# A two-layer selective-scan block: a new load and head, constants made by GpSimd, and unread products on TensorE

## The chip, the cores and the metric

The kernel runs on one core of one Trainium2 chip. The metric is the device time of one execution in microseconds (us), the median of several runs; lower is better. Names used below: TensorE (PE; its weight loads are PEld in the profile), VectorE (DVE), ScalarE (ACT), GpSimd (POOL) and SyncE (SP, which here only issues DMAs). SBUF is the on-chip memory and PSUM the accumulator memory that TensorE writes, which this kernel takes in banks of 512 floats per partition.

## The reference

The input x is an image of 64 x 64 pixels with 96 channels, so L = 4096 tokens. Two layers of the same kind follow each other, each with a residual connection:

```
x = x + conv_block_0(group_norm(x))
x = x + conv_block_1(group_norm(x))

# a block, d = 192 inner channels, n = 16 states
xz = x @ in_proj                      # 96 -> 2 * 192
x_val, z = split(xz)
x_val = silu(depthwise_conv_3x3(x_val))
# four orders of the tokens (by rows, by columns, each forward and backward)
for each order s:
    dt, B, C = split(s @ x_proj)      # 6, 16, 16
    dt = softplus(dt @ dt_proj + bias)
    h[t] = h[t-1] * exp(dt * A) + dt * s * B      # 192 x 16 states
    y_s = sum_n h * C + s * D
y = layer_norm(sum of the four y_s, put back in order) * silu(z)
return y @ out_proj
```

Layer 0 writes its scan as a cumulative sum divided by a decay with 1e-12 added, so that what lies far from the start of an order is swamped and only its first steps count. Group norm has 32 groups of 3 channels.

## The kernel before

Tokens lie along the free dimension and channels on the partitions. The 192 inner channels by 4096 tokens are three blocks of 128 partitions by 2048 columns; a partition half of 64 holds 64 channels for one half of the 512-token chunks.

**Load** (L155 to 163): eight transfers bring x in tiles of 128 tokens by 4 by 96; TensorE turns them four at a time into a PSUM bank, and DVE copies the bank to xT (96 x 4096). Four `xt` buffers are in rotation. DVE also makes the constants from the identity (L95 to L142: `fold`, `fold2`, `wide`, `i3`, `selh`, `less`). `selh` is a bf16 selection matrix, 96 x 1024: a product with 128 of its columns as weights spreads a row of B over 128 partitions.

**Head** (`head`, once a layer): bn_stats (L1347 in layer 0, L1322 behind the residual in layer 1), bn_aggr (L1141), a small product `pm` (L1143) that averages over the groups, three DVE steps, a product `pv` (L1149), Ln and Exp on ACT for the reciprocal deviation `rs`, and eight DVE instructions for the normalised `xn` (L1156). `project` and `borders` (L1163, L1181) are the in-projection; ACT copies it into a padded image (L1167, L1185). The depthwise convolution has twelve parts (three blocks by four chunks): DVE does blocks 0 and 1, two chunks at a time, as nine scaled additions (`conv`, L1237 and L1239); TensorE does block 2, chunk by chunk, as nine products with diagonal weights (`conv_by_products`, L1216). `finish` applies SiLU and starts y. `gate` (L1193 to L1199) computes silu(z) in twelve parts, `sz`, and stores them in DRAM through three buffers.

**Near part** (`near_scans`, layer 0): only the first 192 steps of each order are computed. TensorE selects the tokens (`nu`, L276 to L289), projects them (`npj`, L300), and expands dt (`npd`, L334). ACT and DVE make softplus of it (Abs, Exp, Identity, Ln at L347 to L350, then L351 to L354). Nine bf16 products spread B over the partitions (`nB`, L412 and L414, four PSUM banks, of which 2048 columns are there and the last 256 are free). Six units follow, two for each block: ACT makes decays (`nna`) and weights (`nnwt`), DVE multiplies B and du into `nb` (L467, L474) and scans (L475), POOL multiplies by C (L480), TensorE sums over the states (`ny`, L494), and DVE adds to y after every second unit (L518). After the second unit `reach` (L388 to L399) computes a flag that says whether 192 steps are enough, by a transpose `worst` (L397); the full scans of layer 0, `far_scans`, stand behind a branch on that flag and don't run on this input.

**Tail**: layer norm, the product with silu(z) and the out-projection with the residual.

**Layer 1's scans** (`scans`; nearly all of the span): eight groups of 24 units. All operations go through `Ordered`, a helper that keeps the written order on each engine, so the profile gives all of them the line L668 of that helper. The first group has a start of its own (`first`): `pj` projects, `xd` copies, `pd` expands dt, `tB` transposes B, then on ACT four softplus steps for each of three blocks (`wl`, `w`), with the copy `BT` of tB and the decays `am` (L226) after the second block's steps, then `a` (stage_a), the casts of B to three bf16 parts with the products `less` between, and the transposes `tu`. After that DVE's scans (`h`) run.

What sets the order: outside `Ordered` parts and `keep_in_program_order` the order on an engine is chosen by a scheduler from due times; every engine runs its own queue in order. A reader of a tile waits for the last write to that tile that stands ahead of it in the program, so tiles that share a PSUM tile share waits.

```
            ps = pps.tile([128, 4, 512], F32, tag="B", name="npd")[:, 0:3, 0 : 2 * NEAR]
...
            nc.scalar.activation(w, ps, AF.Abs)
...
                    ps = me["ps"] = spare(f"tB{k}", "v" if k else "b0")
```

Of the kernel before, what the change touches and what calls it, by code (L numbers as in the profile page):

```python
# [16 lines left out]
HW = 64  # L17
L = HW * HW
DM = 96
# [24 lines left out]
def two_ss2d_layers(  # L44
# [43 lines left out]


    load_exp_ln()  # L90
    ident = const.tile([128, 128], F32, name="ident")
    make_identity(nc, ident)

# [5 lines left out]
    for half in HALF:  # L99
        nc.vector.tensor_add(fold[:, half], ident[:, HALF[0]], ident[:, HALF[1]])  # L100
    fold2 = const.tile([128, 128], F32, name="fold2")
    nc.vector.tensor_scalar_mul(fold2, fold, 0.5)

    wide = []
    for h in range(2):
        t = const.tile([128, 128], F32, name=f"wide{h}")
        nc.vector.memset(t, 0.0)
        for half in HALF:
            nc.vector.tensor_copy(t[HALF[h], half], ident[HALF[h], HALF[h]])
        wide.append(t)  # L110
# [9 lines left out]
    nc.sync.dma_start(out=gav, in_=gavg)  # L120
# [4 lines left out]
    nc.vector.tensor_add(i3, ident[0:NB, 0:32], ident[0:NB, 32:64])  # L125
    nc.vector.tensor_add(i3, i3, ident[0:NB, 64:96])
    selh = const.tile([NB, NS, 2, 64], BF16, name="selh")
    for h in range(2):
        nc.vector.tensor_copy(
            selh[:, :, h, :],  # L130
            i3.rearrange("p (q two) -> p q two", two=2)[:, :, h]
            .unsqueeze(2)
            .to_broadcast([NB, NS, 64]),
        )
# [7 lines left out]
    nc.vector.tensor_scalar_mul(less, ident[0:NB, 0:NB], -1.0)  # L142


    u = [pers.tile([128, L // 2], F32, name=f"u{T}") for T in range(3)]
    y = [pers.tile([128, L // 2], F32, name=f"y{T}") for T in range(3)]
    xs = dpool.tile([DM, L], F32, name="xs")
    szd = [dpool.tile([3, 128, L // 2], F32, name=f"szd{l}") for l in range(2)]


    xp = ExitStack()
    xT = xp.enter_context(tc.tile_pool(name="xT0", bufs=1)).tile([DM, L], F32, name="xT0")
    with tc.tile_pool(name="ld", bufs=4) as ld, tc.tile_pool(
        name="ldp", bufs=4, space=PSUM
    ) as ldp:  # L155
        xr = x.rearrange("(g j p) c -> g p j c", p=128, j=4)
        for g in range(8):
            xt = ld.tile([128, 4, DM], F32, tag="xt", name=f"xt{g}")
            (nc.sync if g % 2 == 0 else nc.scalar).dma_start(out=xt, in_=xr[g])
            pt = ldp.tile([DM, 512], F32, tag="pt", name=f"pt{g}")  # L160
            for j in range(4):
                nc.tensor.transpose(pt[:, j * 128 : (j + 1) * 128], xt[:, j, :], ident)
            nc.vector.tensor_copy(xT[:, g * 512 : (g + 1) * 512], pt)
# [82 lines left out]
    def near_scans(weights):  # L246
# [4 lines left out]
        WN = 4 * NEAR  # L251
        with ExitStack() as sc:
# [19 lines left out]
            for T in range(3):  # L272
                ps = pps.tile(
                    [128, 4 if T == 2 else 2, 512], F32, tag="ymB"[T], name=f"nu{T}"
                )[:, 0:2]
                nc.tensor.matmul(  # L276
                    ps[:, 0, 0:NEAR], wide[0], u[T][:, 0:NEAR], start=True, stop=True
                )
                nc.tensor.matmul(
                    ps[:, 0, NEAR : 2 * NEAR], wide[1], u[T][:, L // 2 - NEAR :][:, ::-1],  # L280
                    start=True, stop=True,
                )
                for h in range(2):
                    nc.tensor.matmul(
                        of_columns(ps[:, 1, 0:NEAR], h), wide[h],
                        columns(u[T], h, slice(0, k)), start=True, stop=True,
                    )

                    nc.tensor.matmul(  # L289
                        of_columns(ps[:, 1, NEAR : 2 * NEAR], 1 - h), wide[h],  # L290
                        columns(u[T], h, slice(HW - k, HW))[:, ::-1, ::-1, ::-1],
                        start=True, stop=True,
                    )
                (nc.scalar.copy, nc.vector.tensor_copy)[T % 2](us[:, T], ps[:, :, 0 : 2 * NEAR])
# [3 lines left out]
            for T in range(3):  # L298
                for q in range(2):
                    nc.tensor.matmul(  # L300
                        ps[:, q], xw[HALF[q], 0, T, :], us[HALF[q], T, q],
                        start=(T == 0), stop=(T == 2),
                    )
# [27 lines left out]
            ps = pps.tile([128, 4, 512], F32, tag="B", name="npd")[:, 0:3, 0 : 2 * NEAR]  # L331
            for T in range(3):
                for h, half in enumerate(HALF):
                    nc.tensor.matmul(  # L334
                        ps[half, T], dwb[96 : NC + 1, 0, T, half],
                        xd[96 : NC + 1, 2 * NEAR * h : 2 * NEAR * (h + 1)], start=True, stop=True,
                    )
            w, ln, t, v, sums = (
# [47 lines left out]
            def reach():  # L386
                for i, (n, m0, m1) in enumerate(kinds):
                    nc.vector.tensor_mul(  # L388
                        top[:, i],
                        S.rearrange("p t q (d w) -> p t (q d) w", w=NEAR)[:, :, :, n - 1],  # L390
                        most[:, i, :].unsqueeze(2).to_broadcast([128, 3, 4]),
                    )
                nc.vector.reduce_max(
                    most[:, len(kinds), 0:1], top.rearrange("p i a b -> p (i a b)"), axis=AX.X
                )
                ps = pps.tile([128, 2, 512], F32, tag="m", name="worst")
                nc.tensor.transpose(ps[0:1, 0, 0:128], most[:, len(kinds), 0:1], ident)  # L397
                nc.vector.reduce_max(most[0:1, len(kinds), 1:2], ps[0:1, 0, 0:128], axis=AX.X)
                nc.vector.tensor_scalar(flag, most[0:1, len(kinds), 1:2], GONE, None, ALU.is_le)  # L399
# [5 lines left out]
            for n, m0, m1 in kinds:  # L405
                B.append([])
                t = once.tile([128, m1 - m0, 4 * n], F32, name=f"ncb{n}")
                for m in range(m0, m1):
                    dst = Bf[:, at : at + 4 * n]
                    if n == NEAR:  # L410
                        for s in (slice(0, 512), slice(512, WN)):
                            nc.tensor.matmul(dst[:, s], pick(0, m), B3[:, s], start=True, stop=True)  # L412
                    else:
                        nc.tensor.matmul(  # L414
                            dst.rearrange("p (d w) -> p d w", w=n), pick(0, m),
                            parts(B3)[:, :, 0:n], start=True, stop=True,
                        )
# [5 lines left out]
                cb.append(t.rearrange("p n w -> p (n w)"))  # L423

# [58 lines left out]
            def add(j):  # L483
# [6 lines left out]
                for i in ks:  # L490
                    n, m0, m1 = kinds[i]
                    for m in range(m0, m1):
                        for q in range(2):
                            nc.tensor.matmul(  # L494
# [4 lines left out]
                            o += 2 * n  # L499
                if ks[0]:  # L500
# [153 lines left out]
    def scans(weights):  # L654
# [5 lines left out]
        class Ordered:  # L660
            def __init__(self, engine):
                self.engine = engine

            def __getattr__(self, name):
                op = getattr(self.engine, name)


                return lambda *args, **more: tc.keep_in_program_order(op(*args, **more))  # L668

# [3 lines left out]
        with ExitStack() as sc:  # L673
# [4 lines left out]
            load_exp_ln()  # L678
# [30 lines left out]
            def prelude(k):  # L709
# [48 lines left out]
                def tokens_B():  # L758

                    ps = me["ps"] = spare(f"tB{k}", "v" if k else "b0")  # L760
# [155 lines left out]
            def first(  # L916
# [6 lines left out]
                for h in range(2):  # L923
                    projected(h)
                rows()
                for begin, by_scalar, by_vector in parts:
                    begin()
                tokens_B()
                for T, (begin, by_scalar, by_vector) in enumerate(parts):
# [193 lines left out]
    def head(l, xT, w):  # L1123

        ipw_s, v, ds = w["ipw"], w["v"], w["ds"]
        with ExitStack() as sc:
# [12 lines left out]
            gst = cv.tile([DM, 6], F32, name=f"gst{l}")  # L1139
            gm, rs = gst[:, 2:3], gst[:, 5:6]  # L1140
            nc.vector.bn_aggr(gst[:, 0:2], w["st"].rearrange("p a b -> p (a b)"))  # L1141
            pm = cvp.tile([DM, 1], F32, tag="z", name=f"pm{l}", bufs=3)
            nc.tensor.matmul(pm, gav, gst[:, 0:1], start=True, stop=True)  # L1143
# [5 lines left out]
            nc.tensor.matmul(pv, gav, gst[:, 4:5], start=True, stop=True)  # L1149
            nc.scalar.activation(rs, pv, AF.Ln, bias=eps5[0:DM])  # L1150
            nc.scalar.activation(rs, rs, AF.Exp, scale=-0.5)

            xn = cv.tile([DM, L], F32, name=f"xn{l}")
            for g in range(8):
                s = slice(g * 512, (g + 1) * 512)
                nc.vector.tensor_scalar(xn[:, s], xT[:, s], gm, rs, ALU.subtract, ALU.mult)  # L1156
# [68 lines left out]
            def conv(b, s):  # L1225


                room = cw.tile([128, 2, SR, W2], F32, tag="acc", name=f"acc{l}_{b}_{s}")
                acc = room.rearrange("p c r w -> p c (r w)")[:, :, 0 : SR * W2 - 2]
                for k, (i, j) in enumerate(taps):  # L1230
                    o = i * W2 + j
                    src = pad[b].rearrange("p c r w -> p c (r w)")[
                        :, 2 * s : 2 * s + 2, o : o + SR * W2 - 2
# [6 lines left out]
                finish(b, slice(1024 * s, 1024 * (s + 1)), room[:, :, :, 0:HW])  # L1240
# [11 lines left out]
            conv(0, 0)  # L1252
            for c in range(NCH):
                conv_by_products(2, c)
            for b, s in ((1, 0), (0, 1), (1, 1)):
                conv(b, s)
# [88 lines left out]
    st = [pers.tile([DM, 8, 6], F32, name=f"st{l}") for l in range(2)]  # L1345
    for g in range(8):
        nc.vector.bn_stats(st[0][:, g, :], xT[:, g * 512 : (g + 1) * 512])  # L1347
    nc.sync.dma_start(out=xs, in_=xT)
    for l in range(2):
# [11 lines left out]
        nc.vector.reduce_sum(ds, v[:, :, V_D : V_D + 4], axis=AX.X)  # L1361
# [97 lines left out]
```

## Time and profile before

| | us |
|---|---|
| median of 3 runs | 1553.86 (1553.56 to 1554.03) |
| the profiled execution | 1545.96 |
| its span in the profile | 1543.8 |
| mean granted TensorE clock | 0.913 of full |
| DVE busy, whole span | 1354.3 (88%) |
| first scan of layer 0's near part (L475) | starts at 127.08 |
| tail of layer 0 (first m) | starts at 179.67 |
| bn_aggr of layer 1 | starts at 222.90 |
| first pj of layer 1 | starts at 289.95 |
| first scan of layer 1 (h) | starts at 317.03 |

A line of the timeline reads: start, busy time, engine, source line, operation, written tile <- read tiles, shape, and in brackets the idle time of that engine ahead of it with what ended it. Consecutive instructions of one kind are one line, and "x12" is their number; the busy time is then that of all of them. A matmul of floats is recorded as several passes, so that the records of TensorE are more than the products written in the code. The clock (PEclk) is the share of full speed that TensorE was granted; in short windows of this profile it is 0.50 or 1.00, and a mean over a longer window lies between. The profiled execution is one single run, some 8 us shorter than the median of the timed ones.

### The profile page before, as it was taken

The page shows a single profiled execution, that of the slowest core. Times are in us where ns is not written, and L with a number is a line of the kernel's source. Part 1 is how long each engine was busy: PE and PEld are TensorE (multiplying, and loading weights), DVE is VectorE, ACT ScalarE, POOL GpSimd, SP SyncE. Part 2 cuts the span into 40 slices and gives each one's busy share as a digit, 9 for nine tenths or more (in the row PEclk, how much of TensorE's full clock was granted, in tenths as well). Part 3 has the DMA queues.
Part 4 walks back from the last instruction along what each step waited for, and adds up shares of the span by engine and source line. Part 5 has one row for each costly group of instructions (what it writes and reads, how often), then busy time and mean ns, then how long its engine had stood idle before and what let it go on. Part 6 is the DMA issues. An engine that isn't in the chain of part 4 may idle for free.

```text
span 1543.8 us, 17370 instructions
## 1 busy us (share of the span) xinstructions
PE 1258.3 (82%) x5158; PEld 507.0 (33%) x5158; DVE 1354.3 (88%) x942; ACT 1196.7 (78%) x2459; POOL 1102.9 (71%) x593
## 2 busy tenths in 40 slices
PE   5953779798897888798888889797979888877778
PEld 3432424233332323232323333333333332322223
DVE  6936389469999999999999999999999999999976
ACT  3456125669989898898999999999898989897733
POOL 0032100149898999899898989898989899998860
PEclk8975689869999999998999999999999899999999
DMA  4031330441625344352626162526263544526223
GB/s 111 11 107 45 89 87 1 127 106 37 144 74 133 82 111 108 85 126 68 151 55 153 55 138 57 137 57 146 65 140 76 124 97 96 123 70 146 74 81 96
DMA packets 82674, 146.32 MB, mean 95 GB/s; under 512 B 31580, under 2 KB 33820, under 8 KB 82476
## 3 DMA queue, kind: packets, MB, share of 16 engines
q1 hardware_dynamic: 79884, 142.78, 38.2%
q0 software_dynamic: 576, 1.57, 0.4%
q10 hardware_dynamic: 2112, 0.79, 0.2%
q8 instruction: 42, 0.69, 0.2%
q14 instruction: 60, 0.49, 0.1%
HBM read 80.85 MB, written 12.13 MB: 60 GB/s over the span
## 4 chain that ended last, share of the span: by engine, by line
DVE 26%; issue 21%; PE 13%; ACT 11%; POOL 7%; DMA 6%; SPq 5%; DVEq 0%; POOLq 0%; ACTq 0%
DVE h L668 17%; DVE b L668 6%; POOL hc L668 5%; SPq L668 5%; ACT a L668 4%; PE ys L668 3%; ACT bT L668 2%; PE pj L668 2%; PE b L668 2%; PE cp L1216 2%; DMA cb<-C 2%; DMA du<-su 2%; DMA xT<-xs 1%; PE pd L668 1%; PE in L1163 1%
## 5 line engine op out<-in xcount | busy, mean ns | idle before, releaser
L668 POOL TENSOR_TENSOR hc<-h,cb 128x1024 f32<-128x1024 f32 x384 | 902.7, 2367 | 116.3 <-DVE h L668 61.8
L668 DVE TENSOR_TENSOR_SCAN h<-a,carry,b 128x1024 f32<-128x1024 f32 x288 | 665.2, 2337 | 30.3 <-PE b L668 6.4
L668 ACT ACTIVATE a<-dt,am 128x1024 f32<-128x1024 f32 x384 | 438.6, 1142 | 94.3 <-DVE h L668 91.3
L668 PE MATMUL ys<-hc,fold 128*64 128x512 f32 x1536 | 434.2, 645 | 2.6 <-POOL hc L668 2.6
L668 ACT ACTIVATE bT<-duT,BT 128x192 f32<-128x192 f32 x1012 | 387.2, 445 | 8.3 <-PE b L668 6.4
L668 PE MATMUL b<-ident,bT 128*128 128x128 f32 x1536 | 223.5, 289 | 34.3 <-DVE h L668 27.4
L668 DVE TENSOR_TENSOR b<-b,du 128x1024 f32<-128x1024 f32 x192 | 232.2, 1209 | 12.3 <-PE b L668 12.3
L668 PEld LDWEIGHTS b<-ident,bT 128*128 128x128 f32 x1536 | 176.6, 147 | 160.9 <-DVE h L668 99.1
L668 DVE TENSOR_TENSOR_SCAN h<-a,b 128x1024 f32<-128x1024 f32 x96 | 216.1, 2278 | 13.9 <-PE b L668 6.0
L668 PE MATMUL b<-B,selh 96*128 96x512 bf16 x384 | 122.4, 402 | 90.0 <-DVE h L668 89.9
L668 PEld LDWEIGHTS ys<-hc,fold 128*64 128x64 f32 x1536 | 79.0, 140 | 142.2 <-issue 102.8
L668 PEld LDWEIGHTS <-selh 96*128 96x128 bf16 x384 | 25.9, 98 | 220.9 <-DVE h L668 124.1
L668 PE MATMUL pj<-u,xw 64*124 64x512 f32 x192 | 94.2, 636 | 3.1 <-ACT sz L1198 1.7
L668 PE MATMUL pd<-xd,dwb 29*64 29x512 f32 x192 | 58.2, 677 | 47.0 <-DVE w L668 40.1
L1239 DVE SCALAR_TENSOR_TENSOR acc<-pad,v,acc 128x1052 f32<-128x1052 f32 x64 | 79.6, 1308 | 0.2
L668 POOL DMA_DIRECT2D du<-su x12 | 6.4, 538 | 81.7 <-ACT am L226 79.7
L668 PE MATMUL ys<-y,ident 128*128 128x512 f32 (+1 forms) x120 | 64.7, 646 | 0.0
L1216 PE MATMUL cp<-pad,diag 128*128 128x512 f32 x144 | 62.3, 593 | 0.0
L668 ACT CAST B<-pj 96x512 bf16<-96x512 f32 (+2 forms) x96 | 54.9, 575 | 4.5 <-PE pj L668 4.5
L668 POOL TENSOR_TENSOR sp<-sp,ln 128x512 f32<-128x512 f32 x45 | 57.4, 1275 | 0.2
L668 POOL TENSOR_TENSOR ln<-ln,w 128x512 f32<-128x512 f32 x45 | 57.4, 1276 | 0.0
L668 POOL TENSOR_TENSOR su<-sp,u 128x512 f32<-128x512 f32 x45 | 57.3, 1274 | 0.0
(173 smaller groups left out, 1173.7 us busy)
## 6 DMA issues: line engine op xcount, KB each, us to landing
cb<-C SPq DMA_DIRECT2D x256, 256.0 KB, 4.1
dt<-sp SPq DMA_DIRECT2D x192, 128.0 KB, 4.2
du<-su SPq DMA_DIRECT2D x180, 128.0 KB, 4.2
szd<-sz SPq DMA_DIRECT2D x24, 256.0 KB, 3.1
szt<-szd SPq DMA_DIRECT2D x24, 256.0 KB, 6.8
xT<-xs SPq DMA_DIRECT2D x8, 384.0 KB
xs<-xT SPq DMA_DIRECT2D x1, 1536.0 KB
xs<-xT SPq DMA_DIRECT2D x8, 192.0 KB, 2.3
```

Of the source, the lines that this page charges most:

```text
L668: return lambda *args, **more: tc.keep_in_program_order(op(*args, **more))
L1163: nc.tensor.matmul(ps[half], ipw_s[:, 64 * b : 64 * b + 64], xn[:, g * 512 : (g + 1) * 512], start=True, stop=True,)
L1216: nc.tensor.matmul(ps.rearrange("p (r w) -> p r w", w=HW), diag[:, k, :], pad[b][:, c, i : i + SR, j : j + HW], start=(k == 0), stop=(k == ...
L1239: nc.vector.scalar_tensor_tensor(acc, src, wk, acc, ALU.mult, ALU.add)
```

## The change

The load is written anew, and stands ahead of the constants: each partition reads 1536 contiguous bytes of x, there are eight buffers, ACT makes the copy to xT with a stride of four, and DVE takes bn_stats from PSUM:

```diff
+    with tc.tile_pool(name="ld", bufs=8) as ld, tc.tile_pool(
+        name="ldp", bufs=4, space=PSUM
+    ) as ldp:
+        xr = x.rearrange("(g p j) c -> g p j c", p=128, j=4)
...
+            (nc.sync if g % 2 == 0 else nc.scalar).dma_start(out=xts[g], in_=xr[g])
...
+                nc.tensor.transpose(pt[:, j], xts[g][:, j, :], ident)
+            nc.scalar.copy(
+                xT[:, g * 512 : (g + 1) * 512].rearrange("c (p j) -> c j p", j=4), pt
+            )
+            tc.keep_in_program_order(
+                nc.vector.bn_stats(st[0][:, g, :], pt.rearrange("c j p -> c (j p)"))
+            )
```

`fold`, `fold2`, the copies in `wide`, `i3`, `selh` and `less` go from nc.vector to nc.gpsimd. The transfer of `gav` and the store of xT stand behind that in the text. A new function issues products whose result nothing reads:

```diff
+    def warm(ps, n):
+        for i in range(n):
+            tc.keep_in_program_order(
+                nc.tensor.matmul(
+                    ps, pick(0, 0), selh.rearrange("p q a b -> p (q a b)")[:, 0 : ps.shape[-1]],
+                    start=True, stop=True,
+                )
+            )
```

They are called in the head, where xn is also split between DVE and ACT:

```diff
+            filler = cvp.tile([128, HT], F32, tag="ed", name=f"warm{l}")
+            warm(filler, 8)
             pm = cvp.tile([DM, 1], F32, tag="z", name=f"pm{l}", bufs=3)
...
+            warm(filler, 3)
...
+            warm(filler, 4)
             nc.scalar.activation(rs, pv, AF.Ln, bias=eps5[0:DM])
             nc.scalar.activation(rs, rs, AF.Exp, scale=-0.5)
+            nc.vector.scalar_tensor_tensor(shift, gm, -1.0, rs, ALU.mult, ALU.mult)
...
+                if g % 2 == 0:
+                    nc.vector.tensor_scalar(xn[:, s], xT[:, s], gm, rs, ALU.subtract, ALU.mult)
+                else:
+                    nc.scalar.activation(xn[:, s], xT[:, s], AF.Identity, bias=shift, scale=rs)
```

in the near part, whose products all go through `Ordered` now:

```diff
-            ps = pps.tile([128, 4, 512], F32, tag="B", name="npd")[:, 0:3, 0 : 2 * NEAR]
+            room = pps.tile([128, 4, 512], F32, tag="B", name="npd")
+            ps = room[:, 0:3, 0 : 2 * NEAR]
...
+            warm(room[:, 3], 32)
...
+            filler = Bf[:, 2048 - 256 :]
+            warm(filler, 110)
...
+                if j + 1 < len(units):
+                    warm(filler, 16)
```

and in layer 1's first group:

```diff
-            load_exp_ln()
             am = []
...
-                    ps = me["ps"] = spare(f"tB{k}", "v" if k else "b0")
+                    ps = me["ps"] = spare(f"tB{k}") if k else me["room"][:, halves[0]]
...
                     projected(h)
+                load_exp_ln()
                 rows()
                 for begin, by_scalar, by_vector in parts:
                     begin()
+                room = state[0]["room"] = pps.tile([128, TC], F32, tag="b0", name="room")
                 tokens_B()
+                warm(room[:, halves[1]], 30)
```

The last chunk of block 2's convolution goes from TensorE to DVE, as DVE's last one:

```diff
-            conv(0, 0)
-            for c in range(NCH):
+            conv(0, slice(0, 2))
+            for c in range(NCH - 1):
                 conv_by_products(2, c)
-            for b, s in ((1, 0), (0, 1), (1, 1)):
-                conv(b, s)
+            for b, c in ((1, 0), (0, 2), (1, 2)):
+                conv(b, slice(c, c + 2))
+            conv(2, slice(NCH - 1, NCH))
```

The sum `ds` of the skip weights moves from ahead of the head into it, behind xn.

## The prediction

> **What bounds the kernel.** I read the page's busy sums first, then the timeline of 0 to 346 us, then short windows with the granted clock.
>
> ```profile
> PE 1258.3 (82%) x5158; PEld 507.0 (33%) x5158; DVE 1354.3 (88%) x942; ACT 1196.7 (78%) x2459; POOL 1102.9 (71%) x593
> DVE  6936389469999999999999999999999999999976
> PEclk8975689869999999998999999999999899999999
> ```
>
> DVE is full from the tenth slice on (layer 1's scans), and the change doesn't touch those. It touches the first nine slices, where DVE waits. So each edit is priced by how far it moves the chain there; a delay or a gain at the first scan of layer 1 (317.03) goes to the end unchanged, because DVE has no slack behind it. The chain, from the timeline:
>
> ```profile
> 16.51 4.24 DVE L1347 BATCH_NORM_STATS2 st<-xT 96x6 f32<-96x512 f32 x7
> 20.79 0.37 DVE L1141 BATCH_NORM_AGGREGATE gst<-st 96x2 f32<-96x48 f32 x1
> 32.02 0.77 DVE L1237 TENSOR_SCALAR acc<-pad,v 128x1052 f32<-128x1052 f32 x1 [4.68 <-ACT pad L1185]
> 89.06 0.59 PE L276 MATMUL nu<-u,wide 128*128 128x192 f32 x2 [1.62 <-ACT sz L1198]
> 102.44 1.13 ACT L347 ACTIVATE nw<-npd 128x1152 f32<-128x1152 f32 x1
> 111.64 0.80 PE L412 MATMUL nB<-nB,selh 96*128 96x512 bf16 x2 [9.24 <-DVE nv L353]
> 121.51 0.97 DVE L467 TENSOR_TENSOR nb<-nB,ndu 128x768 f32<-128x768 f32 x1 [2.35 <-DMA ndu<-ndu]
> 126.02 0.96 DVE L474 SCALAR_TENSOR_TENSOR nb<-nnwt,nb 128x768 f32<-128x768 f32 x1 [0.49 <-ACT nnwt L447]
> 153.59 5.38 PE L494 MATMUL ny<-nnhc,fold 128*128 128x64 f32 x24 [1.05 <-POOL nna L453]
> ```
>
> Each line gives the start, the busy time and, in brackets, the idle time ahead of it with what ended it. The reader is to see which lines follow each other without slack (102.44 stands 0.03 behind the end of npd at 102.41) and which have some (nB ends at 113.3, and the nb that reads it starts at 121.51): an added wait costs its length less that slack. In the last line PE is the late one: DVE's y add waits until 159.01 for these 24 products.
>
> **Part by part** (shifts in us against before; negative is earlier).
>
> 1. Load. Before, DVE makes constants (6.42 to 9.2), copies and then does seven bn_stats in 4.24, and the second half of the transposes starts at 12.22. After, all eight transfers are issued at once and DVE only does bn_stats from PSUM, behind ACT's copy. PE is then the bound: 16 transposes took 3.62, so 32 take 7.2 from about 4.0; with a copy (0.6 like ACT's pad rows) and a bn_stats (0.68) the aggregate starts at 12.8 instead of 20.79: **-8.0**. Ends: 11.5 (transposes partly at full clock) to 15.7 (the stride-4 copy on ACT at twice its 0.6, eight of them in line); I take 0.6 because nothing shows a slower one. The constants on POOL lie under this: POOL has 14.63 us idle before its pads, against some 3 us of DVE work moved to it; only selh is wanted soon, by the first filler. On SP's queue gav is still second and the store of xT falls one place back, behind small weight loads that nothing reads before 96 us; the last two transfers of x wait for the first two to land (4.49), 5 us ahead of their transposes. If they came 2 us late, that is inside the upper end.
>
> 2. Norm. Eight unread products stand before pm and wait for the last bn_stats; 512-column bf16 products took 0.43 at half clock and half of that at full, so 8 take 1.7 to 3.4, of which 0.4 to 0.5 lies under the aggregate. The three and four fillers behind pm and pv delay pv and the first `in` product only if they outlast DVE's four small steps (0.78) and ACT's Ln, Exp and shift (1.04): 1.3 and 1.7 at half clock, so up to 0.5 each, none at full. The added DVE shift costs 0.2 (rows of 96x1: 0.15). The diag products on ACT (2.74, nine) now follow its copies and end near 15, ahead of pv. **+2.2** (+1.2 to +4), -5.8 in all.
>
> 3. xn to conv. 23.61 to 32.02 is 8.41. Four xn go to ACT (0.6 each), which delays its pads, and the clock, half until 29.6, should be full earlier: 7.0 (6.5 to 9). **-1.4**, -7.2.
>
> 4. Conv to nu. 57.0 before: PE runs the conv products of block 2 (36, as 72 records, 43.05 to 74.2), then z; sz is bound by its stores to 89.0. After, 54 records (23.4), so z starts 7.8 sooner, at conv start + 34.3, and the 14.9 us from z to nu end at +49.2. DVE gets one more conv of half width: 0.45 and eight of 0.69 to 0.74 (the 128x512 rows of layer 1) are 6.3, so it ends at 42.6 + 6.3 = +48.9, then SiLU and y on ACT. The two are level, and what is late next is ACT: u (1.15) and y (1.15) of the last blocks stand among the twelve sz, and npj needs all of u. I take 51.2. **-5.8** (-2.5 to -7.8), -13.0.
>
> 5. 32 products behind npd. They write the fourth bank of npd's PSUM tile, and the built program's instruction list shows that ACT's Abs (102.44) now waits for the last of them, not for the last npd. Abs had started 0.03 after npd. Queued behind it on ACT are Exp, Identity, Ln, the next table load and the dt copies, and DVE's nv chain waits for those; nothing else on the path can run meanwhile. Four us at half clock (9), the rest at full: **+8.9** (6.8 all full, 13.7 all half). The 9.24 us of idle PE before nB stay, so the clock is not kept.
>
> 6. 110 products behind nB, in nB's tile: DVE's first nb (121.51) waits for the last. nb may start as late as 125.05 without delaying 126.02. Nine nB products take 1.66, then about 11 fillers of 256 columns at 0.21 and 99 at 0.107: nB + 15 to 16 = 127.0. **+1.7** (0 to +11.8 if all are at 0.21).
>
> 7. Near units. 24 small ny at half clock (0.224 each) took 5.38 and DVE waited 5.19, 4.18 and 8.45 for them. At full clock they would take about 3.1 (0.13 each: at 151.82, with the clock full, four weight loads of the same kind took 0.52). Against that, sixteen fillers of 256 columns (1.7 to 3.4) after each unit but the last stand on PE before the worst transpose (DVE's reduce and all its later nb wait there) and before the next ny, and as they write nB's tile, they wait for DVE's latest nb and the next nb for them. The keeping of program order on PE itself moves nothing here: the ny already ran in that order. **-3.3** (-4.5 to +3).
>
> 8. Layer 1's norm and conv: as 2 to 4, with xn split: **-1.4** (-2.6 to +0.5) and 55.4 becoming 50.4, **-5.0** (-2 to -6). In all -12.1 at pj (289.95).
>
> 9. First group.
>
> ```profile
> 298.39 1.06 PE L668 MATMUL tB<-ident,xd 32*128 32x32 f32 x8
> 300.57 0.24 ACT L668 COPY BT<-tB 128x128 f32<-128x128 f32 x1
> 301.77 0.60 ACT L668 ACTIVATE wl<-pd 128x512 f32<-128x512 f32 x1
> 306.15 1.15 ACT L668 ACTIVATE a<-dt,am 128x1024 f32<-128x1024 f32 x1 [1.75 <-DMA dt<-sp]
> 307.20 1.04 ACT L668 CAST B<-pj 96x512 bf16<-96x512 f32 x2
> 307.82 1.07 PE L668 MATMUL pj<-B,less 96*96 96x512 bf16 x2 [8.37 <-ACT B L668]
> 309.93 2.77 PE L668 MATMUL tu<-ident,su 128*128 128x128 f32 x12
> ```
>
> The 30 fillers share tB's tile, so the copy BT waits for the last: 299.45 + 8.5 = 308.0, 7.45 later. Behind it on ACT stand am, the third softplus, a, and the casts that less and tu need. a had 1.75 of idle, of which 1.5 is used: **+5.95** (+3.8 all full, +10.3 all half) and 0.13 for the table load, which stood under pj (289.92, ending 1.67 before xd could start) and now stands behind the two xd copies, where ACT had 1.16 of idle before wl for its 1.28. PE then idles some 6 us again until less. Could the clock stay full to 346, DVE's waits there (1.92 + 3.99 + 2.24 + 1.20) would mostly go, -8.
>
> ```profile
> core 0: us, PE busy (x) PEld busy (x) DVE busy (x) ACT busy (x) POOL busy (x), PEclk, DMA share, GB/s
> 104.00:111.00 7.00, 0.00 (x0) 0.00 (x0) 5.09 (x7) 4.45 (x4) 4.55 (x5) 0.50 0.49 135
> 111.60:113.40 1.80, 1.65 (x9) 1.00 (x9) 1.76 (x2) 0.47 (x1) 0.43 (x1) 0.50 0.07 6
> 316.90:322.40 5.50, 5.50 (x8) 1.86 (x8) 4.56 (x3) 1.72 (x4) 3.00 (x2) 0.50 0.60 161
> ```
>
> The third window has PE busy in all of its 5.50 us, on 64-row products, at clock 0.50: a busy PE was not enough, so I give no part of the 8. The Trainium skill ("TensorE: Matmul & The Clock Gate", Part 1) lifts the clock after about 3.4 us of sustained work, whatever it is; by that rule this window would have been lifted and the sum would be up to 8 lower. The row differs, and the row decides.
>
> **Sum**: -8.0 + 2.2 - 1.4 - 5.8 + 8.9 + 1.7 - 3.3 - 1.4 - 5.0 + 5.95 + 0.13 = -6.0. The profiled execution took 1545.96 us, 7.9 below the median of 1553.86; both move alike, so 1539.9 there and **1547.9** as a median.
>
> **Rivals.** (a) Slower: the fillers never lift the clock. One mechanism, the 0.43 us per 512 columns: terms 5, 6, 7 and 9 become 13.7, 11.8, +3 and 10.3, the sum +19.6, 1573. Linear between 0.28 per 512 columns (the 8.9) and 0.43, it decides from 0.31. For it: clock 0.50 under 64-row and 29-row products. Against: 96-row `in` products lifted it at 29.6 after 5.4 us, and fillers have 96 rows. 0.15. (b) The load gains little: the strided copy bounds it, and sz and DVE's longer conv keep nu where it was plus 2; terms 1, 4 and 8 lose 2.9, 2 and 1.5: about 1554, no change. 0.18. (c) The clock lasts through the first group: 8 from the waits there and 2 at BT: 1538. 0.12. The forecast keeps 0.55, nine tenths of it faster by over 0.2% (3.1 us, what a measurement can tell from no change).
>
> Faster is 0.48 + 0.03 of (b) + 0.12 = 0.63; same 0.07 + 0.10 = 0.17; slower 0.15 + 0.05 = 0.20. The range, 1538 to 1562, takes in (b), (c) and the single bounds of steps 1, 4, 6 and 7; it leaves out (a).
>
> **What would show it.** Aggregate near 12.8, first conv near 24.7, nu near 76; ACT's Abs released by a filler some 9 us after npd; BT's copy by one some 7.5 us late; clock full at the end of each filler run, half again at nB and at pj 64x512. A load bounded by the copy, or fillers at 0.43 throughout, would make it wrong.

## The result, and the profile after

Measured side by side in 20 runs each, the kernel before took 1550.41 us and the changed one 1544.38 us (medians). The medians lie 6.0 apart. The ratio, which goes by the means (1550.34 and 1545.56), is 0.9969 with a 95% interval of 0.9951 to 0.9987: 4.8 us faster, between 2.0 and 7.6. The forecast was 6.0 faster. The profiled execution has a span of 1539.6 us against 1543.8.

The lines of the changed kernel's timeline that answer to those of before. The near part's products now go through `Ordered`, so they carry that helper's line, L97; L189 is the unread product. `top` is the first DVE instruction that reads the transferred nS:

```profile
14.93 0.37 DVE L1171 BATCH_NORM_AGGREGATE gst<-st 96x2 f32<-96x48 f32 x1
29.63 0.77 DVE L1285 TENSOR_SCALAR acc<-pad,v 128x1052 f32<-128x1052 f32 x1 [7.19 <-ACT pad L1231]
77.74 8.19 PE L97 MATMUL nu<-u,wide 128*128 128x192 f32 x36 [2.72 <-ACT sz L1244]
91.36 7.08 PE L189 MATMUL npd<-selh 96*128 96x512 bf16 x32
98.48 1.13 ACT L380 ACTIVATE nw<-npd 128x1152 f32<-128x1152 f32 x1 [6.62 <-PE npd L189]
106.25 1.65 PE L97 MATMUL nB<-nB,selh 96*128 96x512 bf16 x9 [7.80 <-DVE nv L386]
107.69 13.73 PE L189 MATMUL nB<-selh 96*128 96x256 bf16 x110
121.47 0.34 DVE L421 TENSOR_TENSOR top<-nS,most 128x12 f32<-128x12 f32 x3 [7.69 <-DMA nS<-nS]
122.01 0.97 DVE L503 TENSOR_TENSOR nb<-nB,ndu 128x768 f32<-128x768 f32 x1
148.17 5.18 PE L97 MATMUL ny<-nnhc,fold 128*128 128x64 f32 x24 [1.06 <-POOL nna L489]
```

nu comes 11.3 us earlier than before, Abs only 4.0, because it is released by the last of the 32 unread products (`<-PE npd L189`) instead of by the last npd (91.43). The second set of small sums, ny, still takes 5.18 at half clock. The first group of layer 1, with the pj of the kernel before as the first line:

```profile
289.95 3.80 PE L668 MATMUL pj<-u,xw 64*124 64x512 f32 x12 [1.69 <-ACT sz L1198]
274.60 7.21 PE L97 MATMUL pj<-u,xw 64*124 64x512 f32 x12 [3.49 <-ACT sz L1244]
286.37 9.31 PE L189 MATMUL room<-selh 96*128 96x512 bf16 x30
295.71 0.27 ACT L97 COPY BT<-room 128x128 f32<-128x128 f32 x1 [6.83 <-PE room L189]
299.46 1.13 ACT L97 ACTIVATE a<-dt,am 128x1024 f32<-128x1024 f32 x1
301.11 1.07 PE L97 MATMUL pj<-B,less 96*96 96x512 bf16 x2 [5.44 <-ACT B L97]
```

pj starts 15.4 us earlier than before, the first scan of layer 1 (310.15 against 317.03) only 6.9. ACT idles 6.83 ahead of BT, and the twelve records of pj need 7.21 where they took 3.80. Windows of the changed kernel, as before with the clock behind the busy times:

```profile
91.40:94.80 3.40, 3.40 (x17) 1.53 (x17) 1.99 (x5) 0.44 (x2) 3.21 (x4) 1.00 0.22 64
101.30:104.00 2.70, 0.00 (x0) 0.00 (x0) 1.49 (x2) 2.68 (x3) 0.00 (x0) 0.50 0.02 2
153.40:156.80 3.40, 3.40 (x17) 2.53 (x16) 1.88 (x6) 0.00 (x0) 0.00 (x0) 0.50 0.00 0
310.00:315.50 5.50, 5.50 (x8) 1.84 (x8) 4.58 (x3) 1.91 (x4) 2.98 (x2) 0.50 0.76 168
```

The 32 run at full clock; by 101.3, under 3 us after their end, the clock is half again, with the nine nB still to come. In the third window sixteen unread products run at half, though TensorE is busy without a gap; a window of 148.50 to 158.50 has it busy in all of its 10.00 us at 0.50. In the fourth 64-row products do so again.

Stage by stage, each step's length in us (before; after; and the runs below, one profiled execution each; what bears on the argument from e7, e8 and e9 is told at their place):

| step | before | after | e1 | e2 | e3 | e4 | e5 | e6 | e10 |
|---|---|---|---|---|---|---|---|---|---|
| start to bn_aggr | 20.79 | 14.93 | 13.94 | 13.93 | 15.00 | 12.66 | 12.62 | 12.38 | 11.95 |
| to first conv | 11.23 | 14.70 | 11.94 | 14.71 | 10.59 | 10.59 | 10.59 | 10.59 | 10.59 |
| to nu | 57.04 | 48.11 | 46.92 | 47.70 | 57.00 | 47.58 | 48.00 | 47.99 | 47.65 |
| to the end of npd | 13.35 | 13.69 | 12.82 | 12.84 | 11.68 | 13.40 | 13.01 | 11.66 | 11.67 |
| to Abs | 0.03 | 7.05 | 0.46 | 0.45 | 7.05 | 7.05 | 0.46 | 0.46 | 0.46 |
| to nB | 9.20 | 7.77 | 9.28 | 9.29 | 7.76 | 7.76 | 9.28 | 9.28 | 9.28 |
| to the first near scan | 15.44 | 17.90 | 15.43 | 15.39 | 18.50 | 17.92 | 15.43 | 15.44 | 15.47 |
| to the last y (units) | 47.51 | 45.18 | 46.40 | 42.87 | 46.36 | 42.80 | 47.17 | 46.00 | 45.06 |
| to bn_aggr, layer 1 | 48.31 | 47.77 | 48.18 | 48.71 | 48.13 | 48.59 | 48.28 | 47.46 | 48.31 |
| to first conv | 11.69 | 9.49 | 11.84 | 9.49 | 9.49 | 9.49 | 9.49 | 9.49 | 9.49 |
| to pj | 55.36 | 48.01 | 48.02 | 47.96 | 55.80 | 48.02 | 47.86 | 47.89 | 47.93 |
| to wl | 5.58 | 9.15 | 8.77 | 7.71 | 5.74 | 7.68 | 10.07 | 6.65 | 6.61 |
| to a | 10.62 | 15.71 | 10.71 | 10.53 | 15.72 | 14.19 | 10.58 | 10.27 | 10.51 |
| to the first scan of layer 1 | 10.88 | 10.69 | 10.87 | 10.74 | 10.86 | 10.67 | 10.88 | 10.88 | 10.88 |
| that scan's start | 317.03 | 310.15 | 295.58 | 292.32 | 319.68 | 298.40 | 293.72 | 286.44 | 285.86 |

The start of that scan is the measure below, because behind it the executions differ by more than most of the steps: from there to the end of the span it is 1226.8 us before, 1229.4 in the changed kernel (its lead of 6.9 is 4.2 in the span), and 1220.7 (e7) to 1234.6 (e9) over all twelve profiles. DVE's busy time there is 1148.2 to 1149.0 in all of them; what differs is its idle time, 72 to 86. The 20 timed runs of the changed kernel spread as far (1538.33 to 1551.99).

### The profile page after: what moved, and what is told of

It reads as the page before. It is cut to its first block, busy times and chain, and to the rows that moved or that the text cites. A ratio compares the mean times of both kernels' runs of the same rounds, so it can differ in the third digit from the quotient of the medians.

```text
span 1539.6 us, 17893 instructions
## 1 busy us (share of the span) xinstructions
PE 1285.3 (83%) x5404; PEld 525.8 (34%) x5404; DVE 1353.9 (88%) x934; ACT 1209.8 (79%) x2475; POOL 1107.8 (72%) x605
## 3 DMA queue, kind: packets, MB, share of 16 engines
q0 software_dynamic: 576, 1.57, 0.4%
## 4 chain that ended last, share of the span: by engine, by line
DVE 27%; issue 22%; PE 13%; ACT 9%; POOL 6%; DMA 6%; SPq 5%; DVEq 0%; POOLq 0%; ACTq 0%
DVE h L97 17%; DVE b L97 7%; SPq L97 5%; POOL hc L97 4%; ACT a L97 4%; PE ys L97 3%; DMA cb<-C 3%; PE b L97 2%; ACT bT L97 2%; PE pd L97 2%; PE pj L97 2%; PE cp L1262 2%; DVE w L97 1%; DMA du<-su 1%; POOL ln L97 1%
## 5 line engine op out<-in xcount | busy, mean ns | idle before, releaser
L97 POOL TENSOR_TENSOR hc<-h,cb 128x1024 f32<-128x1024 f32 x384 | 903.2, 2368 | 115.5 <-DVE h L97 61.2
L97 DVE TENSOR_TENSOR_SCAN h<-a,carry,b 128x1024 f32<-128x1024 f32 x288 | 665.0, 2337 | 30.0 <-PE b L97 9.1
L97 ACT ACTIVATE a<-dt,am 128x1024 f32<-128x1024 f32 x384 | 438.5, 1142 | 92.6 <-DVE h L97 91.4
L97 PE MATMUL ys<-hc,fold 128*64 128x512 f32 x1536 | 433.9, 645 | 2.6 <-POOL hc L97 2.6
L97 ACT ACTIVATE bT<-duT,BT 128x192 f32<-128x192 f32 x1012 | 387.0, 445 | 7.8 <-PE b L97 5.8
L97 PE MATMUL b<-ident,bT 128*128 128x128 f32 x1536 | 223.4, 289 | 33.8 <-DVE h L97 26.9
L97 DVE TENSOR_TENSOR b<-b,du 128x1024 f32<-128x1024 f32 x192 | 232.2, 1209 | 12.7 <-PE b L97 12.7
L97 PEld LDWEIGHTS b<-ident,bT 128*128 128x128 f32 x1536 | 176.4, 147 | 160.8 <-DVE h L97 98.4
L97 DVE TENSOR_TENSOR_SCAN h<-a,b 128x1024 f32<-128x1024 f32 x96 | 216.1, 2278 | 13.7 <-PE b L97 5.4
L97 PE MATMUL b<-B,selh 96*128 96x512 bf16 x384 | 122.4, 402 | 89.7 <-DVE h L97 89.2
L97 PEld LDWEIGHTS ys<-hc,fold 128*64 128x64 f32 x1536 | 78.9, 140 | 141.2 <-issue 98.5
L97 PEld LDWEIGHTS <-selh 96*128 96x128 bf16 x393 | 26.9, 99 | 230.5 <-DVE h L97 126.0
L97 PE MATMUL pj<-u,xw 64*124 64x512 f32 x192 | 97.6, 665 | 4.9 <-ACT sz L1244 3.5
L97 PE MATMUL pd<-xd,dwb 29*64 29x512 f32 x192 | 57.6, 673 | 49.6 <-DVE w L97 42.8
L1287 DVE SCALAR_TENSOR_TENSOR acc<-pad,v,acc 128x1052 f32<-128x1052 f32 (+1 forms) x80 | 91.4, 1200 | 0.7
L97 POOL DMA_DIRECT2D du<-su x12 | 6.4, 537 | 82.7 <-DVE su L97 82.7
L97 PE MATMUL ys<-y,ident 128*128 128x512 f32 (+1 forms) x120 | 62.9, 630 | 0.0
L97 ACT CAST B<-pj 96x512 bf16<-96x512 f32 (+2 forms) x96 | 54.9, 575 | 4.2 <-PE pj L97 4.2
L97 POOL TENSOR_TENSOR sp<-sp,ln 128x512 f32<-128x512 f32 x45 | 57.5, 1278 | 0.2
L97 POOL TENSOR_TENSOR ln<-ln,w 128x512 f32<-128x512 f32 x45 | 57.6, 1280 | 0.0
L97 POOL TENSOR_TENSOR su<-sp,u 128x512 f32<-128x512 f32 x45 | 57.4, 1275 | 0.0
L97 PEld LDWEIGHTS pj<-u,xw 64*124 64x124 f32 x192 | 35.1, 199 | 64.4 <-issue 44.9
```

Of the source, the lines that this page charges most:

```text
L1287: nc.vector.scalar_tensor_tensor(acc, src, wk, acc, ALU.mult, ALU.add)
```

## The experiments

Theory A: an unread product costs its time wherever a reader waits for its PSUM tile, and the clock it buys is worth less than that. Rival B: the products pay for themselves. All kernels below are the changed one with an edit; ratios are against the kernel before.

**e1, no unread product.**

```diff
-        for i in range(n):
+        for i in range(0):
```

> The changed kernel without any unread product (nothing else differs). Theory A (an unread product costs its time wherever a reader waits for its PSUM tile or a useful product stands behind it, and the clock it buys is worth less): against the changed kernel's profile the first convolution of layer 0 starts 2.4 us earlier (27.2 instead of 29.6), ACT's Abs another 7 earlier (near 89 instead of 98.5, within 0.1 us of the last npd), the near part loses some 3 us again because its 24 small sums run at half clock (2.9 become 5.2 to 5.4 us), BT's copy in the first group comes 7 us after less, and layer 1's first scan starts near 298 instead of 310.2; the time is some 10 to 12 us under the changed kernel's, about 1533. Rival B (the products pay for themselves by the clock): the first scan of layer 1 starts at 308 or later and the time is equal to the changed kernel's or above.

1528.5 us, ratio 0.988 (0.9858 to 0.9902): 16 us under the changed kernel by the medians, 14 by the two ratios (10 to 12 expected). The scan starts at 295.58, 14.6 earlier (2.4 more than the 12 expected). Abs stands 0.46 behind npd instead of 7.05. The units lose 1.2, not the 3 expected: their small sums fall to half clock, but no queue of sixteen stands before them. B falls: the rest of the change is worth 21.5 us at this scan, and the kernel with the products stands 14.6 behind that (1.0 of it in the load, where none of them stands).

**e2, tiles that nothing reads.** The products stay; the 32 and 110 go to another tile, and ACT makes BT's copy behind the first casts of B.

```diff
-            warm(room[:, 3], 32)
+            idle = pps.tile([128, 2, 512], F32, tag="y", name="idle")
+            warm(idle[:, 0], 32)
...
-            warm(filler, 110)
+            warm(idle[:, 1, 0:256], 110)
...
-                        tokens_B_out()
                         am.extend(decays(weights[2]))
...
                     first_part(h)
+                tokens_B_out()
```

> The changed kernel with the 32 and the 110 unread products of the near part written to a PSUM tile that nothing reads at that time, and with BT's copy in the first group moved on ACT behind the casts of B (so that nothing on ACT waits for the 30 products early). All products stay. Theory A (the wait through the shared tile is the cost, not the products): Abs starts within 0.1 us of the last npd, near 91.5 instead of 98.5; the first nb no longer stands behind the 110; in the first group a starts near 286 instead of 299.5 in its own frame, and the products less start when the 30 end; layer 1's first scan starts 11 to 14 us earlier than the changed kernel's, near 297; the time is about 1532. Rival B (Abs and BT are late for another reason, a table load, a transfer or the clock): Abs still starts 6 us or more behind npd, and the time moves by less than 3 us.

ACT's timeline of this run, at npd (which ends at 89.18) and in the first group:

```profile
89.15 0.46 ACT L256 ACTIVATE am<-ab 64x24 f32<-64x24 f32 x2
89.63 1.13 ACT L381 ACTIVATE nw<-npd 128x1152 f32<-128x1152 f32 x1
```

```profile
281.58 1.15 ACT L97 ACTIVATE a<-dt,am 128x1024 f32<-128x1024 f32 x1 [1.82 <-DMA dt<-sp]
283.57 0.27 ACT L97 COPY BT<-room 128x128 f32<-128x128 f32 x1
```

Neither Abs nor the first nb nor `a` waits for an unread product any more; `a` waits for the transfer of dt, as in the kernel before. The sixteen behind each unit still write nB's tile, and a later nb waits 1.57 for them. The scan starts at 292.32, 17.8 earlier than the changed kernel's (11 to 14 expected); 1528.25 us, ratio 0.9873 (0.9852 to 0.9895). The shared tile is the cost, as A has it: Abs 7.05 to 0.45, the first near scan 17.90 to 15.39 (by a way of its own, see step 6 below), wl to a 15.71 to 10.53. Freed of the waits, the products win a little at this mark: 3.3 us against e1, from the units, layer 1's head and pj, less the 2.8 that they cost in the first head (14.71 against 11.94). The times don't show it.

**e3, the convolution's last chunk back on TensorE.**

```diff
-            for c in range(NCH - 1):
+            for c in range(NCH):
                 conv_by_products(2, c)
...
-            conv(2, slice(NCH - 1, NCH))
```

> The changed kernel with the last chunk of block 2's convolution back on TensorE, in both layers. Theory A (the moved chunk lets z and so the twelve sz start 7.8 us earlier, and DVE's longer convolution ends level with them): nu starts 5 to 7 us later than the changed kernel's from the same start of the convolution (48.1 after it becomes 54), and layer 1's first pj likewise (48.0 becomes 54); layer 1's first scan starts 10 to 13 us later. Rival B (the gain between convolution and nu comes from elsewhere, the order of u among the sz or the faster clock): nu stays within 2 us of 48.1 after the first convolution.

57.00 and 55.80 from convolution to nu and pj, as before (57.04, 55.36): the moved chunk alone is worth 8.9 and 7.8, where about 6 each was expected. The time, 1551.15 us, is that of one run. The scan starts 9.5 later than the changed kernel's (10 to 13 expected), since other steps differ: pj takes 5.74 to wl here and 9.15 there, and the first head 10.59 and 14.70. That last pair is the same code. In this run the products of the first head got full clock:

```profile
15.00 0.37 DVE L1171 BATCH_NORM_AGGREGATE gst<-st 96x2 f32<-96x48 f32 x1
15.02 1.89 PE L189 MATMUL warm<-selh 96*128 96x512 bf16 x8 [2.15 <-DVE st L129]
```

In the changed kernel's profile they started at 14.94 and took 3.25. Its granted clock was 0.56, 0.50 and 0.57 in three windows from 14.9 to 26.2, where e3 had 1.00 in every window from 14.9 to 26.0. So 4.1 us of the head hang on the moment at which the clock changes, not on the code.

**e4, contiguous copies in the load.**

```diff
-        xr = x.rearrange("(g p j) c -> g p j c", p=128, j=4)
+        xr = x.rearrange("(g j p) c -> g p j c", p=128, j=4)
...
-                xT[:, g * 512 : (g + 1) * 512].rearrange("c (p j) -> c j p", j=4), pt
+                xT[:, g * 512 : (g + 1) * 512].rearrange("c (j p) -> c j p", j=4), pt
```

> The changed kernel with the old order of tokens in the load (each partition reads 384 bytes four times, ACT's copy to xT writes contiguous columns); eight buffers, bn_stats from PSUM and all else as changed. In the changed kernel bn_aggr starts at 14.93, 2.1 us later than forecast. Theory A (ACT's copy with a stride of four is the cause: 0.93 us each instead of 0.6): the copy takes 0.6 us, TensorE's transposes follow each other at 0.9 per bank, and bn_aggr starts near 12.8 if the transfers land as early. Rival B (the transfers are the cause: TensorE waited 1.76 for the third one until 7.43): bn_aggr stays at 14.5 or later, or comes later still because the shorter pieces of 384 bytes move more slowly.

ACT's copies in the changed kernel and, in the second fence, in this run:

```profile
8.56 5.60 ACT L125 COPY xT<-pt 96x512 f32<-96x512 f32 x6 [1.73 <-PE pt L124]
```

```profile
8.26 0.58 ACT L125 COPY xT<-pt 96x512 f32<-96x512 f32 x1 [0.27 <-PE pt L124]
12.66 0.37 DVE L1171 BATCH_NORM_AGGREGATE gst<-st 96x2 f32<-96x48 f32 x1
```

0.93 each becomes 0.58, ACT now waits 0.27 for TensorE where its last six copies had followed each other without a gap, and bn_aggr starts at 12.66, the forecast's 12.8. Theory A holds: the four profiles with the stride have 13.93 to 15.00 here, the seven without it 11.65 to 12.66. The transfers also landed earlier (24 of the transposes from 6.28 instead of 7.43), so B has a share that this run does not part from it. The scan starts 11.8 earlier; of that 2.3 is the load, 4.1 the first head's clock, 2.4 the units and 3.0 the first group (9.15 to 7.68, 15.71 to 14.19), whose code is the same. The time, 1527.54 us, is that of one run.

**e5 to e8, on top of the contiguous copies.** e5 keeps the unread products of the heads and drops all others; e8 drops those as well; e6 is e5 with products in the gap between the last z and nu or pj; e7 is e5 with the 32 and 110 in the tile that nothing reads (as in e2).

```diff
             for b in range(3):
                 for c in range(NCH):
                     gate(b, c)
+            last = cvp.tile([128, HT], F32, tag="ed", name=f"last{l}")
+            warm(last, (12, 16)[l])
```

> The changed kernel with contiguous copies in the load (as in the run with the plain copy) and with unread products in the two heads alone; those of the near part and of the first group are gone. Theory A (each wait through a shared tile is removed, and the waits add): against the run with the plain copy, Abs comes 7.0 us earlier, of which DVE gives back 1.4 because it shares its time with POOL again; nB to the first near scan 17.9 becomes 15.4; the units lose their queue of sixteen, 42.8 becomes about 41.7; the first group's wl to a, 14.2, becomes 10.7: layer 1's first scan at about 285 (298.4 minus 13), the time near 1518. Rival B (the runs without products differ by the phase of the clock, not by the waits): layer 1's first scan within 5 us of 298.

> As the run with products in the heads only, plus unread products (12 in layer 0, 16 in layer 1, into a tile that nothing reads) between the last z and the first nu or pj, where TensorE waited 2.7 and 3.5 us for ACT's last sz. Theory A (an unread product helps where its gap is short, nothing waits for it and 64-row work follows): the twelve records of pj take 3.8 to 4.5 us instead of 7.2, so wl starts 3 us earlier behind the first pj; layer 1's first scan 3 us earlier than without them, the time 2 to 4 us lower. Rival B (64-row products lose the clock in any case, or the products end late): pj still takes over 6.5 us, or starts later by more than it saves, and the first scan doesn't move by more than 1 us.

> As the run with products in the heads only, plus the 32 and the 110 of the near part, written to a PSUM tile that nothing reads at that time. Theory A (the clock that they buy is worth next to nothing there, because the late engines are ACT, DVE and the transfers, and TensorE only takes nine products of 1.65 us off the path): from npd to the last y of the near part the two runs agree within 1.5 us, and the times agree within their interval. Rival B (the clock is what the products are for): the near part ends 3 us or more earlier than without them, its small sums at 2.9 us instead of 5.2.

> As the run with products in the heads only, without those too: contiguous copies in the load, and no unread product anywhere. Theory A (in the heads nothing late waits for the tile, so what counts there is the clock of the in-projection): bn_aggr to the first convolution 12.0 instead of 10.6 in layer 0 and 11.8 instead of 9.5 in layer 1, so layer 1's first scan 3.7 us later than with them. Rival B (they cost their time ahead of pm in the head as well): both stages are the same or shorter without them, and the time is the same or lower.

e5: 1525.72 us, ratio 0.9854 (0.9812 to 0.9897); the scan at 293.72, 4.7 earlier than in e4 and not 13. The waits went as expected (Abs 6.6, first near scan 2.5, wl to a 3.6), but 1.5 came back between Abs and nB, the units took 47.17 instead of 42.80, and wl came 10.07 behind pj instead of 7.68. So A holds for the waits and fails for the sum, and the scan lies where rival B put it, within 5 us of 298. The moment of the clock has its share: up to pj the code of layer 1 is that of e4, and pj took 5.75 there and 7.39 here. And the sixteen behind each unit do buy something: with them the units took 42.80 to 46.36 in six profiles, without them 46.00 to 47.51 in six.

e6 shows what full clock ahead of pj is worth. TensorE at pj, in e5 and then in e6:

```profile
262.19 7.39 PE L97 MATMUL pj<-u,xw 64*124 64x512 f32 x12 [3.49 <-ACT sz L1238]
```

```profile
254.90 3.63 PE L189 MATMUL last<-selh 96*128 96x512 bf16 x16
258.64 4.72 PE L97 MATMUL pj<-u,xw 64*124 64x512 f32 x12
```

The gap of 3.49 is filled, no reader waits, and pj takes 4.72 instead of 7.39: pj to wl 6.65 instead of 10.07. e5 is the far end of a spread: seven profiles with the gap of 3.49 have pj at 5.75 to 7.39 and wl 7.68 to 10.07 behind its start, three with the gap filled (e6, e9, e10) 4.66 to 4.72 and 6.60 to 6.65. So the filling is worth 1 to 3.5 us. The scan starts at 286.44 (7.3 earlier, 3 expected; the rest is other steps); 1520.62 us, ratio 0.981 (0.978 to 0.9841), an interval that overlaps e5's. The clock in e5's gap, which begins at 258.70:

```profile
258.70:259.20 0.50, 0.00 (x0) 0.00 (x0) 0.47 (x2) 0.50 (x2) 0.00 (x0) 1.00 0.82 307
259.20:260.00 0.80, 0.00 (x0) 0.00 (x0) 0.77 (x2) 0.80 (x1) 0.00 (x0) 0.51 0.07 26
```

The Trainium skill ("TensorE: Matmul & The Clock Gate", section "HAM oscillation — how this bites in real kernels") gives as the rule that TensorE should have no idle gaps of over some 3.4 us. This gap is 3.49 long, but the clock was down half a microsecond into it, and behind the 32 products of the changed kernel it was half again by 101.3, 2.9 us after their end; so these rows don't bear out 3.4 us as the limit.

e7: 1521.16 us, ratio 0.9821 (0.979 to 0.9852), the scan at 291.94. From the end of npd to the last y it took 71.8 against 72.3 in e5, and its units 47.18 against 47.17: the 32 and 110 buy nothing that shows there (0.5), even free of waits. e8: 1528.62 us, ratio 0.9871 (0.9831 to 0.9912). Its heads are 2.1 and 2.4 longer than e5's (12.68 and 11.92), as expected, but other steps were shorter by 3.5 in sum, so the scan came only 1.0 later (3.7 expected). Against e1, which differs from it by the stride alone, its load is 2.3 shorter and its scan 0.9 earlier, and the times can't be told apart.

**e9 and e10, the sixteen behind each unit added to e6**, e9 with the 32 and 110 in the unread tile as well.

> The run with products in the gap (contiguous copies, products in the heads and between the last z and nu or pj), plus the 32 and the 110 of the near part in a tile that nothing reads, plus the sixteen after each unit as in the changed kernel; none in the first group. What is open is why the run with products in the heads only won 4.7 us where 13 were expected: its near units took 47.2 us from the first scan to the last y, against 42.8 with the sixteen. Theory C (the sixteen behind each unit lift the clock for the small sums and are worth 3 to 4 us net, while the 32 and the 110 and the 30 only cost): the near units take 43 to 44 us instead of 46 to 47, layer 1's first scan comes near 283.5 instead of 286.4, the time 2 to 4 us under that of the run with products in the gap, the best of all. Rival D (the 42.8 was a lucky phase of the clock's grid): 45 us or more, and no gain.

> As the run before it, without the 32 and the 110 of the near part: the sixteen after each unit alone. Theory C (the sixteen work by themselves): from the first near scan to the last y 43 to 44 us here too, and the times of the two runs agree within their intervals. Rival E (the sixteen need the 110 ahead of them, which bring TensorE to full clock before the first sums): 45.5 us or more here, with 43 to 44 in the run that has the 110.

e9: 1519.97 us, ratio 0.9812 (0.9792 to 0.9832), units 44.93. e10: 1517.68 us, ratio 0.9819 (0.9788 to 0.9851), units 45.06. The scan starts at 286.09 and 285.86 (C had 283.5, e6 286.44). C misses, and D is nearer: the sixteen gain about 1 us over e6's 46.00, the 110 are not needed for it (E falls), and the 42.8 of e2 and e4 is not reached, so some 2 us of it were probably the moment of the clock. The times of e6, e7, e9 and e10 can't be told apart; at 1.8 to 1.9% under the kernel before, against 0.3% for the changed one, they are the best that was found.

## Why the prediction was right

The direction and the size were right, but that the size came out is partly luck: it is a sum of steps that missed on both sides, and the first head alone hung by 4.1 us on the moment of the clock. At the first scan of layer 1 the forecast's -6.0 stands against -6.88 (nu to npd, +0.3, and the tail of layer 0, -0.5, are not in the table):

| step of the forecast | forecast | profile after |
|---|---|---|
| 1 load | -8.0 | -5.9 |
| 2 norm, 3 xn to conv | +2.2, -1.4 | +3.5 |
| 4 conv to nu | -5.8 | -8.9 |
| 5 Abs behind the 32 | +8.9 | +7.0, then -1.4 to nB |
| 6 the 110 | +1.7 | +2.5 |
| 7 units | -3.3 | -2.3 |
| 8 layer 1: head, conv to pj | -1.4, -5.0 | -2.2, -7.4 |
| 9 first group, table load | +6.1 | +8.5 |

- **1** took 0.6 for ACT's strided copy "because nothing shows a slower one"; it took 0.93, and ACT's copies were the bound, not TensorE's transposes. The upper end (15.7, with 1.2 for the copy) covers the 14.93. e4 shows the forecast's time without the stride.
- **2 and 3** met half clock until 26 in this execution; seven of the runs with products in the head show 10.59 for both steps, better than forecast, and e2 14.71. The size depends on the execution.
- **4 and 8** were too small. DVE's convolution ended 48.9 behind its start, as forecast, but the 2.3 added for ACT's u and y weren't due: nu's first blocks don't read the last u, and the last nu found it ready. z started at +32.3, 2 earlier than thought. e3 shows the whole of it to be the moved chunk.
- **5** held: a wait of 7.05 on the last product. They ran at full clock throughout, the forecast's lower end being 6.8. Not foreseen: by then POOL had finished, and DVE's nt step took 0.76 instead of 2.05, which gave 1.4 back.
- **6** came near in size (its own terms, 127.0 less 125.05, give 1.95 and not 1.7), but the wait that ended last was another. In the changed kernel `top` waits 7.69 for the transfer of nS and stands ahead of nb, while the 110 end at 121.42, level with it. In e4 the 110 ended at 113.70, `top` waited until 114.28, and the step took 17.92 all the same. SP issues the transfers in another order (ndu, ndt, ndu for ndt, ndu), nS lands 15.2 behind nB instead of 13.3, and DVE has `top` ahead of nb. This order stands in the three programs in which the 32 and the 110 write shared tiles (changed kernel, e3, e4) and in none of the others, so the shared tiles brought it, but no run parts the 32 from the 110. That the size came near is luck.
- **7** held: -2.3 against -3.3. The three sets of small ny took 2.89, 5.18 and 4.64 instead of 5.38 each, and the queue of sixteen took part of the gain, as said.
- **9** held for BT (15.71 to 10.53 in e2; 5.1 against the 5.95 forecast). The step that failed is the one that isn't there: 3.6 from pj to wl. With z done earlier, TensorE idled 3.49 for ACT's last sz (1.69 before), and pj ran at a clock of 0.52. e3, with the chunk on TensorE, has a gap of 1.79 and 5.74 there, and e6, with the gap filled, 6.65. So part of step 4's gain went into a new wait.
- The premise that a gain at this scan goes to the end unchanged, "because DVE has no slack behind it", is only roughly so: DVE idles 72 to 86 us behind it, and that differs between executions by more than the whole effect. The means of 20 runs (-4.8) agree with the -6.9 within their interval.

Rival (a) is out: in the changed kernel's profile the 32 took 0.22 us per 512 columns, the 110 0.25, the 30 0.31; at 0.41 or more were only the first head's fifteen and one set of sixteen (3.62). (b) was half true (2.1 of its 2.9), and outweighed by 4 and 8. (c) did not occur: the clock was half at 310 to 315.5.

## What to carry to other kernels

A product issued only to keep TensorE's clock up must write a PSUM tile that no later reader waits for: here the shared tiles turned 7.1 and 5.1 us of filling into waits on the path, and 2.5 more came with the order of transfers that went with them. It pays where TensorE's gap is short and useful products follow at once (with 16 of them pj took 4.7 in three profiles, without them 5.8 to 7.4 in seven), and bought nothing measurable ahead of 9 us in which ACT and DVE work (e7). A stage of one profile can be 4 us off by the moment of the clock alone, so compare several. Price the parts of a bundled change at one common mark late on the path: the -7 at layer 1's first scan hid -21 and +15.

## What the runs showed of the hardware

- The same instructions from the same start took 14.70 and 10.59 us (after and e3, first head): the granted clock was 0.50 to 0.57 in windows from 14.9 to 26.2 in one and 1.00 in the other.
- TensorE busy without a gap isn't enough for full clock: six 64-row records of pj took 5.48 at clock 0.50 in the kernel before, the changed one and e10 alike, and the changed kernel has 10.00 us of busy TensorE at 0.50 (148.5 to 158.5), with ny of 128 rows and products of 96.
- A DVE step of 128x1152 (nt) took 0.76 in the three profiles in which POOL was idle then, and 1.97 to 2.13 beside POOL's work in the other nine. The Trainium skill ("Trainium Architecture — The Big Picture", section "What this means for kernel authors") says that DVE and GpSimd share a port pair by an exclusive lock; these rows fit that, and no run isolates the lock.
- ACT's copy of 96x512 to a stride of four took 0.93, to contiguous columns 0.58.
